# Six of eight layer norms turned by VectorE blocks and copies between partition quarters

## The chip, the cores and the metric

The kernel runs on one core of one Trainium2 chip. Its metric is the device time of one execution in microseconds (us). The core has TensorE (PE, matrix products; its weight loads are shown as PEld), VectorE (DVE), ScalarE (ACT), GpSimd (POOL) and SyncE (SP), whose queue issues nearly all transfers (DMA). Each engine works through its own instructions in the order in which the program gives them, and an instruction that waits holds up those behind it on the same engine. This holds for SP too: a transfer that waits for its data or for its buffer holds up the transfers behind it.

## The reference: what is computed

A cross-attention block with an MLP, for four batches `b`, with L = 512 rows, D = 512 features, 16 heads of 32 and an inner width of 2048, all in float32:

```
xn  = layer_norm(x) * ln1_w + ln1_b                      # LN1
q   = xn @ q_w + q_b ;  k = ctx @ k_w + k_b ;  v = ctx @ v_w + v_b
out = softmax(q k^T / sqrt(32)) v                        # per head
h   = out @ cproj_w + cproj_b + x
y   = layer_norm(h) * ln2_w + ln2_b                      # LN2
out = h + gelu(y @ fc_w + fc_b) @ proj_w + proj_b
```

There are eight layer norms, LN1(b) and LN2(b) for the four batches. Each norm has its rows (positions) on the partitions, four tiles of 128 rows by 512 features, and the products that follow want features on the partitions. So each normed batch, 512 x 512, is turned (transposed), and the norm's weight and bias are applied on the turned side, where they are one scalar per partition.

## The kernel before, in words

**Attention units.** Heads are taken in groups of four: 4 batches x 4 groups give 16 windows `w`, and each window has 4 blocks of 128 query rows, so there are 64 units `u = 4 w + qt`. A unit, in the program's order: perhaps `attend` of an earlier pair, then `scores(w, qt)` (PE into `sc`; VectorE adds the mask and takes the minimum, L284; ScalarE takes exponentials, L288), then `turn(w, qt)` (VectorE transposes the 32 x 32 blocks of the probabilities into `tb`, L302 and L310), then a list of other work that fills PE.

**Pairs and their copies.** A block transpose on VectorE turns only inside blocks of 32 x 32, that is inside a quarter of the partitions. Two units make a pair (pair `2 w + half`), and sixteen SP transfers (`copies`, L345) move its blocks between the four partition quarters from `tb` into `pT`. Then `attend` (L362, `av`) multiplies with `v`, and VectorE scales the result into `oT` (L367). Most pairs, 8 to 24 among them, share one `pT` buffer: their copies are put into SP's order by `exchange`, called in `attend` of the pair before. In the units told of here, an even unit attends pair (u - 4) / 2: unit 20 pair 8, unit 22 pair 9, unit 24 pair 10, and so on to unit 50 and pair 23.

**Filling work.** Preparations `k`, `q`, `v` of window `w` (`prep_k`, `prep_q`, `prep_v`; k9 is that of window 9), output projections `c` (`cproj`, four per batch), and the MLP of batch 0 and half of batch 1 (`fc`, `proj`). Each is one "chain" of PE. Their weights come over SP: `load_w` for `k`, `q`, `v`, two windows ahead, and `load_mlp`, eight tiles ahead. `load_x`, `load_enc` and `load_h` (L194, L189, L391) load a batch's input, context and residual. What fills which unit stands in `first[w]` and `later[w]`. A tuple gives one list for each of the window's four units. Otherwise `run` takes from one list by due times: each chain has a price (CHAIN 3.4, a group of turns TURN 0.5, other steps 0), the sum over the window is divided over its units, and a step is taken while the price spent plus half of its own is within what is due.

**Norms and turns.** `ln_stat` takes mean and variance (VectorE), `ln_rs` the inverse deviation (GpSimd), `ln_norm` the normed rows in place or into a tile of the pool `tiles` (tag `xn`, four buffers), on VectorE or, for LN1(1) and LN1(2), on ScalarE (L163). `ln_turn` then makes a quarter of the turn: four PE transposes of 128 x 128 into PSUM (L176, tile `tp`), and one pass over them with weight and bias, on ScalarE (L181) or VectorE (L179). Four of these make a norm. LN1's turned result is `xT` (a half of the tile `xe`), read by `prep_q`. LN2's is `yT`, one buffer, read by `fc` and in the last phase.

**Last phase.** After the units, `last_mlps` does the second half of batch 1's MLP and those of batches 2 and 3, with fewer products by sums of blocks (L573 and L613). LN2(2) and LN2(3) are turned there, in `project`, after its second product (`turns()`). `y_sums` and the next batch's first products read the result.

Of the kernel before, what the change touches and what calls it, by code (L numbers as in the profile page):

```python
# [1 line left out]

# [9 lines left out]
F32 = mybir.dt.float32  # L38
U8 = mybir.dt.uint8
AF = mybir.ActivationFunctionType  # L40
# [5 lines left out]
P = 128  # L46
B, L, D, H = 4, 512, 512, 16
HD = D // H
INNER = 4 * D
NT = L // P  # L50
ND = D // P
# [5 lines left out]
NI = P // HD  # L57
# [15 lines left out]
LN1W, LN1B, QB, KB, LN2W, LN2B, FCB = 0, 4, 8, 12, 16, 20, 24  # L73
# [4 lines left out]
def xattn_block(ctx: ExitStack, tc: tile.TileContext, x, encT, mask, q_w, k_w, v_w, c_w, fc_w, p_w, vecs, rows, out):  # L78
    nc = tc.nc
    scale = float(np.float32(1.0) / np.sqrt(HD).astype(np.float32))  # L80

    def pools(stack, **bufs):
        return [stack.enter_context(tc.tile_pool(name=n, bufs=k)) for n, k in bufs.items()]

    const, keep, hids, tiles, small = pools(ctx, const=1, keep=1, hids=6, tiles=4, small=4)
    dram = ctx.enter_context(tc.tile_pool(name="dram", bufs=1, space=bass.MemoryType.DRAM))
    ps_acc = ctx.enter_context(tc.tile_pool(name="ps_acc", bufs=4, space=PSUM))

# [6 lines left out]
    vec = const.tile([P, NVEC], F32, tag="vec", name="vec")  # L95
# [9 lines left out]
    eT, xT = (xe[:, i * ND * L : (i + 1) * ND * L].rearrange("p (d l) -> p d l", d=ND) for i in range(2))  # L105
# [9 lines left out]
    def k_q(w, i):  # L115
        n = w % 4 * 2 + i
        return pbt[:, n * D : (n + 1) * D]
# [11 lines left out]
    def kqv_w(w, i):  # L129
        n = 4 * i + 2 + w % 2  # L130
        return ptt[:, n * D : (n + 1) * D].rearrange("p (d f) -> p d f", d=ND)

    S = {}
    count = [0, 0, 0]
    Q = [nc.sync]

    def acc_tile(name):
        return ps_acc.tile([P, D], F32, tag="acc", name=name)


    def ln_stat(key, t, src):
        if t == 0:
            S["mv", key] = small.tile([P, NT, 2], F32, tag="mv", name=f"mv{key[0]}_{key[1]}")
        st = small.tile([P, 6], F32, tag="st", name=f"st{key[0]}_{key[1]}_{t}")
        nc.vector.bn_stats(st, src)
        nc.vector.bn_aggr(S["mv", key][:, t, :], st)

    def ln_rs(key):

        ve = small.tile([P, NT], F32, tag="ve", name=f"ve{key[0]}_{key[1]}")  # L150
        nc.gpsimd.tensor_scalar(ve, S["mv", key][:, :, 1], EPS, 1.0, ALU.add, ALU.mult)
        rs = small.tile([P, NT], F32, tag="rs", name=f"rs{key[0]}_{key[1]}")
        nc.gpsimd.tensor_tensor(rs, ve, nhalf, ALU.pow)
        S["rs", key] = rs
        if key in BY_ACT:
            nm = small.tile([P, NT], F32, tag="nm", name=f"nm{key[0]}_{key[1]}")
            nc.gpsimd.tensor_tensor(nm, S["mv", key][:, :, 0], rs, ALU.mult)
            nc.gpsimd.tensor_scalar(nm, nm, -1.0, 0.0, ALU.mult, ALU.add)
            S["nm", key] = nm

    def ln_norm(key, t, dst, src):
        if key in BY_ACT:
            nc.scalar.activation(  # L163
                dst, src, AF.Identity, bias=S["nm", key][:, t : t + 1], scale=S["rs", key][:, t : t + 1]
            )
            return
        nc.vector.tensor_scalar(
            dst, src, S["mv", key][:, t, 0:1], S["rs", key][:, t : t + 1], ALU.subtract, ALU.mult
        )

    def ln_turn(key, d, xn, dst):

        w, bi = (LN1W, LN1B) if key[0] == 1 else (LN2W, LN2B)
        tp = acc_tile(f"tp{key[0]}_{key[1]}_{d}")
        for t in range(NT):
            nc.tensor.transpose(tp[:, ts(t, P)], xn[t][:, ts(d, P)], ident)  # L176
        wd, bd = vec[:, w + d : w + d + 1], vec[:, bi + d : bi + d + 1]
        if d in (1, 2) and key not in BY_ACT:
            nc.vector.tensor_scalar(dst[:, d, :], tp, wd, bd, ALU.mult, ALU.add)  # L179
        else:  # L180
            nc.scalar.activation(dst[:, d, :], tp, AF.Identity, bias=bd, scale=wd)  # L181


    def queue(b):
        return Q[0] if b else nc.sync

    def load_enc(b):
        for d in range(ND):
            queue(b).dma_start(out=eT[:, d, :], in_=encT[b, ts(d, P), :])  # L189

    def load_x(b):
        S["xn", b] = [tiles.tile([P, D], F32, tag="xn", name=f"xn1_{b}_{t}") for t in range(NT)]
        for t in range(NT):
            queue(b).dma_start(out=S["xn", b][t], in_=x[b, ts(t, P), :])  # L194

# [11 lines left out]
    def ln1_turn(b, d):  # L207
        ln_turn((1, b), d, S["xn", b], xT)
# [167 lines left out]
    def stays(b, t):  # L376

        return b == 0 or b == SPLIT and t < 2

    def load_h(b, *ts_):  # L380

        if ("xa", b) not in S:
            S["xa", b] = dram.tile([L, D], F32, tag=f"xa{b}", name=f"xa{b}")
        for t in ts_:
            if b == B - 1:

                S["h", b, t] = k_q(t // 2, t % 2)
            else:
                pool, tag = (hids, "hid") if stays(b, t) else (tiles, "xn")
                S["h", b, t] = pool.tile([P, D], F32, tag=tag, name=f"h_{b}_{t}")  # L390
            Q[0].dma_start(out=S["h", b, t], in_=x[b, ts(t, P), :])  # L391
            if stays(b, t):
                S["hid", b, t] = S["h", b, t]
# [14 lines left out]
    def load_xn(b):  # L408

        for t in range(NT):  # L410
            S["h", b, t] = tiles.tile([P, D], F32, tag="xn", name=f"hn_{b}_{t}")
            Q[0].dma_start(out=S["h", b, t], in_=S["xa", b][ts(t, P), :])

    def load_hid(b, ts_):
# [8 lines left out]
    def stat2(b, t):  # L423
        ln_stat((2, b), t, S["h", b, t])

    def norm2(b, t):
        h = S["h", b, t]
        y = tiles.tile([P, D], F32, tag="xn", name=f"xn2_{b}_{t}") if stays(b, t) else h
        S.setdefault(("yn", b), {})[t] = y
        ln_norm((2, b), t, y, h)  # L430

    def proj_bias(b):
        for t in range(NT):
            if stays(b, t):
                add_row(S["hid", b, t], 1)

    def ln2_turn(b, d):
        if d == 0:
            S["yT", b] = keep.tile([P, ND, L], F32, tag="yT", name=f"yT_{b}")
        ln_turn((2, b), d, S["yn", b], S["yT", b])  # L440


    weights, products = [], []
# [268 lines left out]
    CHAIN, TURN = 3.4, 0.5  # L712

    def do(fn):
        return [(0.0, fn)]

    def A(w):
        if w >= NW:
            return []
        return [  # L720
            (CHAIN, lambda: prep_k(w)),
            (CHAIN, lambda: prep_q(w)),
            (CHAIN, lambda: prep_v(w)),
        ]

    def C(b):
        return [(CHAIN, lambda t=t: cproj(b, t)) for t in range(NT)]

    def turns1(b):
        return [(TURN, lambda d=d: ln1_turn(b, d)) for d in range(ND)]  # L730

    def turns2(b):
        return [(TURN, lambda d=d: ln2_turn(b, d)) for d in range(ND)]

    def FC(b, q):
        return [(CHAIN, lambda f=f: fc(b, f)) for f in range(q * FQ, (q + 1) * FQ)]
# [3 lines left out]

    def inputs(b):
        ln = [(0.0, lambda part=part: ln1(b, part)) for part in range(3)]
        return do(lambda: load_x(b)), ln, turns1(b), do(lambda: load_enc(b))

    def run(work, budget=None):

# [33 lines left out]
    x1, x2, x3, x4 = inputs(1)  # L780
# [9 lines left out]
    first = [[] for _ in range(NW)]  # L790
    later = [[] for _ in range(NW)]
# [17 lines left out]
    def some(n):  # L809
        taken, mlp[:n] = mlp[:n], []  # L810
        return taken
# [4 lines left out]
    def h_(b, *ts_):  # L816
        return do(lambda: load_h(b, *ts_))
# [4 lines left out]
    def pb_(b):  # L822
        return do(lambda: proj_bias(b))

    def rs(b):
        return do(lambda: ln_rs((2, b)))

    def stat(b, *ts_):
        return do(lambda: [stat2(b, t) for t in ts_])

    def norm(b, *ts_):
        return do(lambda: [norm2(b, t) for t in ts_])


    x1, x2, x3, x4 = inputs(2)
    k, q, v = A(7)
    c, t2 = C(0), turns2(0)
    first[4] = x1 + [k, q, v] + x4
    later[4] = c[:1] + x2[:1] + c[1:2] + x2[1:2] + c[2:3] + x2[2:] + c[3:]
    k, q, v = A(8)  # L840
    first[5] = (
        [k] + stat(0, 0, 1, 2, 3) + rs(0) + x3 + norm(0, 0, 1, 2, 3) + [v], [q] + t2, some(2) + pb_(0), some(2)
    )
    k, q, v = A(9)
    x1, x2, x3, x4 = inputs(3)
    first[6] = [k, q] + some(4) + [v] + x1
    k, q, v = A(10)
    first[7] = [k, q] + x2[:1] + some(2) + x2[1:2] + some(3) + [v]

    k, q, v = A(11)  # L850
    first[8] = h_(1, 0, 1) + x2[2:] + [k, q] + x3[:2] + some(1) + x3[2:3] + [v] + x3[3:] + h_(1, 2, 3) + x4
    later[8] = cb(1) + C(1)
    k, q, v = A(12)
    first[9] = [q] + some(2) + [k] + some(2) + [v]
    k, q, v = A(13)
    first[10] = [k, q] + some(4) + [v]
    k, q, v = A(14)
    t2 = turns2(1)
    first[11] = (
        [k, q] + stat(1, 0, 1, 2, 3) + rs(1), some(2) + norm(1, 0, 1, 2, 3), some(1) + t2[:2] + [v],  # L860
        t2[2:] + pb_(1) + some(1) + h_(2, 2, 3, 0, 1)
    )

    k, q, v = A(15)
    c = C(2)
# [49 lines left out]
    c = C(B - 1)  # L915
# [49 lines left out]
```

## Time and profile before

| | |
|---|---|
| median of 3 runs | 810.5 us (809.81 to 810.87) |
| span of the profiled execution | 810.8 us |
| PE busy | 794.0 us (98%) |
| VectorE, ScalarE, GpSimd busy | 556.1, 359.8, 98.5 us |
| PE transposes of the norms (L176) | 128 instructions, 16 a norm |
| copies of pairs on SP into `pT` (L345) | 384 transfers of 136 KB, 2.4 us from issue to landing |

Times inside the execution are microseconds from the start of the span. A line of the profile names an engine, the source line (L176), the operation and the tiles as out<-in; `[4.15 <-ACT pbt L248]` says that the engine had been idle for 4.15 us and that the operation named ended this. PEclk is TensorE's granted clock, in tenths of full speed. SPq is SP's queue of transfers. The units told of below start, by their `av`, at 153.17 us (unit 20), 196.94 (unit 24), 266.32 (unit 32), 304.38 (unit 36), 389.69 (unit 46) and 421.47 (unit 50).

### The profile page before, as it was taken

What the parts mean: (1) busy time and instruction counts of PE and PEld (TensorE: products, weight loads), DVE (VectorE), ACT (ScalarE), POOL (GpSimd) and SP (SyncE); (2) the same over time, 40 slices, a digit from 0 to 9 for tenths busy, and PEclk for the clock granted to TensorE, in tenths of its full rate; (3) what the DMA queues carried; (4) which work ended last, traced back from release to release, by engine and by line L of the source; (5) the groups of instructions that cost most, each with busy time, mean ns of one, the idle gap of its engine ahead of it and who ended that gap; (6) DMA issues with size and microseconds to landing.
All of it is one profiled execution on the core that took longest, in us unless ns stands there. A gap on an engine that the chain in (4) does not pass through costs nothing.

```text
span 810.8 us, 11918 instructions
## 1 busy us (share of the span) xinstructions
PE 794.0 (98%) x4082; PEld 482.1 (59%) x4082; DVE 556.1 (69%) x1273; ACT 359.8 (44%) x785; POOL 98.5 (12%) x112
## 2 busy tenths in 40 slices
PE   9999999979999999999999999999999999999998
PEld 6545445444354544535554333445888888888887
DVE  3779998876678765867778998636738993358511
ACT  2557765537673646546644469700312330023200
POOL 1110030030000030001131000120050021200011
PEclk9999999989999999999999999999999999999999
DMA  9899999937797877778668798883335330023001
GB/s 332 277 236 221 236 223 243 243 92 186 186 240 173 229 202 201 168 196 210 165 144 219 192 266 222 214 247 127 97 111 175 111 116 14 27 79 91 1 14 39
DMA packets 60956, 137.14 MB, mean 169 GB/s; under 512 B 12464, under 2 KB 15664, under 8 KB 60768
## 3 DMA queue, kind: packets, MB, share of 16 engines
q1 hardware_dynamic: 59472, 132.43, 61.3%
q0 software_dynamic: 896, 2.82, 1.0%
q10 hardware_dynamic: 528, 1.14, 0.6%
q8 instruction: 32, 0.52, 0.3%
q14 instruction: 28, 0.23, 0.1%
HBM read 58.22 MB, written 6.82 MB: 80 GB/s over the span
## 4 chain that ended last, share of the span: by engine, by line
PE 82%; DVE 7%; SPq 4%; ACT 3%; DMA 3%; issue 1%; POOL 0%; DVEq 0%; POOLq 0%; ACTq 0%
PE q L573 15%; PE accf L469 7%; PE accc L403 7%; PE sc L279 7%; PE acck L235 6%; PE av L362 6%; PE accp L479 6%; PE accv L257 6%; PE accq L245 6%; SPq L345 4%; DVE ptt L284 2%; PE q5p L613 2%; PE q3p L613 2%; PE q7p L613 2%; PE q2p L613 2%; PE q6p L613 2%
## 5 line engine op out<-in xcount | busy, mean ns | idle before, releaser
L288 ACT ACTIVATE ptt<-ptt,mn 128x512 f32<-128x512 f32 x256 | 181.6, 711 | 134.2 <-DVE mn L284 134.1
L284 DVE CUSTOM_DVE_ANT_0 ptt<-sc,mb 128x512 f32<-128x512 f32 x256 | 161.1, 685 | 47.5 <-PE sc L279 47.4
L302 DVE STREAM_TRANSPOSE tb<-ptt 128x512 f32<-128x512 f32 x224 | 142.0, 683 | 5.5 <-ACT ptt L288 5.1
L469 PE MATMUL accf<-yT,pbt 128*128 128x512 f32 x192 | 87.3, 602 | 0.0
L479 PE MATMUL accp<-pbt,gt 128*128 128x512 f32 x192 | 86.7, 600 | 0.3 <-DMA pbt<-p_w_dram 0.3
L279 PE MATMUL sc<-pbt 32*128 32x512 f32 x512 | 73.7, 645 | 5.2 <-ACT pbt L248 2.7
L573 PE MATMUL q<-ys,gt 128*128 128x256 f32 x320 | 75.1, 379 | 0.0
L573 PEld LDWEIGHTS q<-ys,gt 128*128 128x128 f32 x320 | 60.9, 190 | 8.2
L469 PEld LDWEIGHTS accf<-yT,pbt 128*128 128x128 f32 x192 | 35.0, 190 | 50.2 <-issue 45.4
L479 PEld LDWEIGHTS accp<-pbt,gt 128*128 128x128 f32 x192 | 35.2, 190 | 49.3 <-issue 45.6
L257 PEld LDWEIGHTS accv<-ptt,xe 128*128 128x128 f32 x512 | 58.9, 192 | 8.2 <-issue 6.9
L257 PE MATMUL accv<-ptt,xe 128*128 128x128 f32 x512 | 60.5, 277 | 0.0
L245 PE MATMUL accq<-xe,ptt 128*128 128x512 f32 x128 | 59.3, 607 | 0.0
L235 PE MATMUL acck<-xe,ptt 128*128 128x512 f32 x128 | 59.3, 606 | 0.0
L573 PE MATMUL q<-yT,gt 128*128 128x256 f32 x240 | 58.1, 380 | 0.5 <-DVE gt L501 0.5
L403 PE MATMUL accc<-wc,oT 128*128 128x512 f32 x128 | 56.6, 596 | 0.0
L269 POOL TENSOR_TENSOR v<-v,row 128x512 f32<-128x512 f32 x16 | 20.4, 1272 | 281.4 <-ACT v L262 281.3
L577 ACT ACTIVATE ga<-uc,vec 128x256 f32<-128x256 f32 x40 | 20.3, 508 | 75.5 <-DVE uc L551 75.5
L573 PEld LDWEIGHTS q<-yT,gt 128*128 128x128 f32 x240 | 45.6, 190 | 7.4 <-DVE gt L501 0.9
L362 PE MATMUL av<-pT,v 128*32 128x256 f32 x768 | 48.1, 393 | 1.5 <-DMA pT<-tb 1.5
L584 ACT COPY p<-q 128x256 f32<-128x256 f32 x20 | 7.1, 353 | 92.0 <-PE q L573 92.0
L288 ACT ACTIVATION_READ_ACCUMULATOR ptt<-ptt,mn 128x1 f32 x256 | 47.8, 187 | 0.0
(121 smaller groups left out, 940.4 us busy)
## 6 DMA issues: line engine op xcount, KB each, us to landing
pT<-tb SPq DMA_DIRECT2D x384, 136.0 KB, 2.4
pbt<-p_w_dram SPq DMA_DIRECT2D x40, 256.0 KB, 3.2
gt<-fc_w_dram SPq DMA_DIRECT2D x40, 256.0 KB, 2.7
gt<-tb SPq DMA_DIRECT2D x64, 136.0 KB, 2.8
xe<-tb SPq DMA_DIRECT2D x56, 136.0 KB, 3.1
pbt<-fc_w_dram SPq DMA_DIRECT2D x24, 256.0 KB, 4.7
ptt<-k_w_dram SPq DMA_DIRECT2D x16, 256.0 KB, 3.8
xe<-encT_dram SPq DMA_DIRECT2D x16, 256.0 KB, 4.3
```

The costliest lines, as they stand in the source:

```text
L235: nc.tensor.matmul(acc, S["wk", w][:, d, :], eT[:, d, :], start=(d == 0), stop=(d == ND - 1))
L245: nc.tensor.matmul(acc, S["wq", w][:, d, :], xT[:, d, :], start=(d == 0), stop=(d == ND - 1))
L257: nc.tensor.matmul(acc[:, ts(t, P)], eT[:, d, ts(t, P)], S["wv", w][:, d, :], start=(d == 0), stop=(d == ND - 1),)
L279: nc.tensor.matmul(sc[:, h, :], qT[r, ts(qt, P)], kT[r, :], start=True, stop=True)
L284: nc.vector.tensor_tensor_reduce(out=s, in0=sc[:, h, :], in1=S["mb", w // NG], scale=1.0, scalar=FMAX, op0=ALU.add, op1=ALU.min, accum_out=mn,
L288: nc.scalar.activation(s, s, AF.Exp, bias=mn, scale=-1.0, accum_out=sums[:, qt, h : h + 1])
L302: nc.vector.transpose(tv[:, q, h], S["ps", w, qt][h])
L362: nc.tensor.matmul(av[ts(h, HD), : 2 * P].rearrange(shape, **kw), v[:, t, ts(h, HD)], p[t][h], start=(t == 0), stop=(t == NT - 1),)
L403: nc.tensor.matmul(acc, S["oT", b][:, g, ts(t, P)], wc[:, g, :], start=(g == 0), stop=(g == NG - 1))
L469: nc.tensor.matmul(acc, S["fcw", b, f][:, d, :], S["yT", b][:, d, :], start=(d == 0), stop=(d == ND - 1))
L479: nc.tensor.matmul(acc, gT[q % 2][:, k, ts(t, P)], S["pw", b, q * FQ + k], start=(k == 0), stop=(k == FQ - 1))
L573: nc.tensor.matmul(o, a[:, k], y[:, k], start=(k == 0), stop=(k == 1))
```

## The change

LN1(0) and LN1(1) stay as they are. For LN1(2), LN1(3) and all four LN2, the turn is made in three steps:

- `ln_flip`: four VectorE transposes (128 x 512 each) turn the 32 x 32 blocks of the normed rows into the destination (`xT` or `yT`).
- `ln_swap`: sixteen SP transfers, each of 32 partitions by 2 KB, move these blocks between the partition quarters, from the destination back into the ring of normed rows. That ring is now one fixed tile `xnt` of four slots instead of a pool.
- `ln_affine`: four ScalarE passes (128 x 512) apply weight and bias, from `xnt` into the destination.

So a norm's ring is in use until its last ScalarE pass; before, it was free after PE's transposes. The steps' prices in the due times are 0, where four groups of turns had 0.5 each.

The order of units 16 to 47 changes with this. Worked out by the due times, the filling work is:

| unit | before | after |
|---|---|---|
| 16, 17 | k7 q7; v7 | k7; q7 v7 |
| 18, 19 | c0 c1; c2 c3 | c0; c1 c2 |
| 20 | k8, statistics of LN2(0), turns of LN1(2), norm of LN2(0), v8 | flip LN1(2), c3, statistics, k8, swap LN1(2) |
| 21 | q8, turns of LN2(0) | a statistic, affine LN1(2), v8 |
| 22 | fc0 fc1 | norm and flip LN2(0), q8, v9, swap LN2(0) |
| 23 | fc2 fc3 | affine LN2(0), k9, q9 |
| 24 to 27 | k9 q9; fc4 fc5; fc6; fc7 v9 | fc0 fc1; fc2 fc3; fc4; fc5 fc6 |
| 28 to 31 | k10 q10; proj0 proj1; proj2 proj3; fc8 v10 | k10 q10; fc7 proj0; proj1 proj2; proj3 v10 |
| 32 | `load_h` (2), norm LN1(3), k11, q11, a turn | the same, flip LN1(3) in place of the turn |
| 33 | turn, fc9, turn, v11 | fc8, swap LN1(3), v11, affine LN1(3), `load_h` (2), `load_enc` |
| 34 | turn, `load_h` (2), `load_enc`, c0, c1 | c0, c1 |
| 36 to 38 | q12 fc10; fc11 k12; proj4 | q12 fc9; fc10 fc11; k12 proj4 |
| 46 | proj8, two turns of LN2(1), v14 | flip LN2(1), proj8, v14, swap LN2(1) |
| 47 | two turns, proj9, `load_h` (4) | affine LN2(1), proj9, `load_h` (4) |

In the last phase, flip, swap and affine of LN2(2) and LN2(3) stand at the place of the turns. The core of the diff:

```diff
-    const, keep, hids, tiles, small = pools(ctx, const=1, keep=1, hids=6, tiles=4, small=4)
+    const, keep, hids, small = pools(ctx, const=1, keep=1, hids=6, small=4)
...
+    xnt = const.tile([P, NT * D], F32, tag="xnt", name="xnt")
+
+    def xn_tile():
+        n = count[3] % NT
+        count[3] += 1
+        return xnt[:, n * D : (n + 1) * D]
...
+    def ln_flip(key, xn, dst):
+
+        tmp = dst.rearrange("p d l -> p (d l)").rearrange("p (j c t q) -> p t c j q", j=NI, c=ND, t=NT)
+        for t in range(NT):
+            nc.vector.transpose(tmp[:, t], xn[t])
+
+    def ln_swap(dst):
+
+        tmp = dst.rearrange("p d l -> p (d l)").rearrange("p (j n) -> p j n", j=NI)
+        for d in range(NI):
+            for i in (0, 2, 1, 3):
+                j = (i + d) % NI
+                nc.sync.dma_start(out=xnt[ts(j, HD), ts(i, D)], in_=tmp[ts(i, HD), j])
+
+    def ln_affine(key, dst):
+
+        w, bi = (LN1W, LN1B) if key[0] == 1 else (LN2W, LN2B)
+        raw = xnt.rearrange("p (i c t q) -> p c t i q", i=NI, c=ND, t=NT)
+        for d in range(ND):
+            nc.scalar.activation(
+                dst[:, d, :].rearrange("p (t i q) -> p t i q", t=NT, i=NI), raw[:, d], AF.Identity,
+                bias=vec[:, bi + d : bi + d + 1], scale=vec[:, w + d : w + d + 1],
+            )
...
-    def ln2_turn(b, d):
-        if d == 0:
+    def ln2_turn(b, step):
+        if step == 0:
             S["yT", b] = keep.tile([P, ND, L], F32, tag="yT", name=f"yT_{b}")
-        ln_turn((2, b), d, S["yn", b], S["yT", b])
+            ln_flip((2, b), S["yn", b], S["yT", b])
+        elif step == 1:
+            ln_swap(S["yT", b])
+        else:
+            ln_affine((2, b), S["yT", b])
...
     k, q, v = A(7)
+    k8, q8, v8 = A(8)
+    k9, q9, v9 = A(9)
     c, t2 = C(0), turns2(0)
     first[4] = x1 + [k, q, v] + x4
-    later[4] = c[:1] + x2[:1] + c[1:2] + x2[1:2] + c[2:3] + x2[2:] + c[3:]
-    k, q, v = A(8)
+    later[4] = c[:1] + x2[:1] + c[1:2] + x2[1:2] + c[2:3] + x2[2:]
     first[5] = (
-        [k] + stat(0, 0, 1, 2, 3) + rs(0) + x3 + norm(0, 0, 1, 2, 3) + [v], [q] + t2, some(2) + pb_(0), some(2)
+        x3[:1] + c[3:] + stat(0, 0, 1, 2) + [k8] + x3[1:2], stat(0, 3) + rs(0) + x3[2:] + [v8],
+        norm(0, 0, 1, 2, 3) + t2[:1] + [q8, v9] + t2[1:2], t2[2:] + pb_(0) + [k9, q9]
     )
-    k, q, v = A(9)
     x1, x2, x3, x4 = inputs(3)
-    first[6] = [k, q] + some(4) + [v] + x1
+    first[6] = some(7) + x1
...
-    first[8] = h_(1, 0, 1) + x2[2:] + [k, q] + x3[:2] + some(1) + x3[2:3] + [v] + x3[3:] + h_(1, 2, 3) + x4
+    first[8] = h_(1, 0, 1) + x2[2:] + [k, q] + x3[:1] + some(1) + x3[1:2] + [v] + x3[2:] + h_(1, 2, 3) + x4
...
-        [k, q] + stat(1, 0, 1, 2, 3) + rs(1), some(2) + norm(1, 0, 1, 2, 3), some(1) + t2[:2] + [v],
+        [k, q] + stat(1, 0, 1, 2, 3) + rs(1), some(2) + norm(1, 0, 1, 2, 3), t2[:1] + some(1) + [v] + t2[1:2],
         t2[2:] + pb_(1) + some(1) + h_(2, 2, 3, 0, 1)
     )
```

In units 20 to 22, `x3` is the list flip, swap, affine of LN1(2), `t2` that of LN2(0), and `some(n)` takes the next n steps of the MLP.

More of the change, by code (lines that the diff above doesn't have):

```diff
@@ L131, in kqv_w @@
         return ptt[:, n * D : (n + 1) * D].rearrange("p (d f) -> p d f", d=ND)
+    xnt = const.tile([P, NT * D], F32, tag="xnt", name="xnt")
[3 more added lines that the diff above has]
+        return xnt[:, n * D : (n + 1) * D]
     S = {}
-    count = [0, 0, 0]
+    count = [0, 0, 0, 0]
     Q = [nc.sync]
@@ L191, in load_x @@
     def load_x(b):
-        S["xn", b] = [tiles.tile([P, D], F32, tag="xn", name=f"xn1_{b}_{t}") for t in range(NT)]
+        S["xn", b] = [xn_tile() for t in range(NT)]
         for t in range(NT):
@@ L388, in load_h @@
             else:
-                pool, tag = (hids, "hid") if stays(b, t) else (tiles, "xn")
-                S["h", b, t] = pool.tile([P, D], F32, tag=tag, name=f"h_{b}_{t}")
+                S["h", b, t] = hids.tile([P, D], F32, tag="hid", name=f"h_{b}_{t}") if stays(b, t) else xn_tile()
             Q[0].dma_start(out=S["h", b, t], in_=x[b, ts(t, P), :])
@@ L410, in load_xn @@
         for t in range(NT):
-            S["h", b, t] = tiles.tile([P, D], F32, tag="xn", name=f"hn_{b}_{t}")
+            S["h", b, t] = xn_tile()
             Q[0].dma_start(out=S["h", b, t], in_=S["xa", b][ts(t, P), :])
@@ L427, in norm2 @@
         h = S["h", b, t]
-        y = tiles.tile([P, D], F32, tag="xn", name=f"xn2_{b}_{t}") if stays(b, t) else h
+        y = xn_tile() if stays(b, t) else h
         S.setdefault(("yn", b), {})[t] = y
@@ L730, in turns1, with flips1 @@
         return [(TURN, lambda d=d: ln1_turn(b, d)) for d in range(ND)]
+    def flips1(b):
+        return [
+            (0.0, lambda: ln_flip((1, b), S["xn", b], xT)),
+            (0.0, lambda: ln_swap(xT)),
+            (0.0, lambda: ln_affine((1, b), xT)),
+        ]
     def turns2(b):
-        return [(TURN, lambda d=d: ln2_turn(b, d)) for d in range(ND)]
+        return [(0.0, lambda n=n: ln2_turn(b, n)) for n in range(3)]
     def FC(b, q):
@@ L742, in inputs @@
         ln = [(0.0, lambda part=part: ln1(b, part)) for part in range(3)]
-        return do(lambda: load_x(b)), ln, turns1(b), do(lambda: load_enc(b))
+        return do(lambda: load_x(b)), ln, turns1(b) if b < 2 else flips1(b), do(lambda: load_enc(b))
     def run(work, budget=None):
@@ L850, in xattn_block @@
     k, q, v = A(11)
-    first[8] = h_(1, 0, 1) + x2[2:] + [k, q] + x3[:2] + some(1) + x3[2:3] + [v] + x3[3:] + h_(1, 2, 3) + x4
+    first[8] = h_(1, 0, 1) + x2[2:] + [k, q] + x3[:1] + some(1) + x3[1:2] + [v] + x3[2:] + h_(1, 2, 3) + x4
     later[8] = cb(1) + C(1)
     k, q, v = A(12)
-    first[9] = [q] + some(2) + [k] + some(2) + [v]
+    first[9] = [q] + some(3) + [k] + some(2) + [v]
     k, q, v = A(13)
```

## The prediction

> **What bounds the kernel now.** I read the page's busy shares first, then TensorE's own instructions in order of time, then the SP queue's, and last the rows of single operations.
>
> ```profile
> span 810.8 us, 11918 instructions
> PE 794.0 (98%) x4082; PEld 482.1 (59%) x4082; DVE 556.1 (69%) x1273; ACT 359.8 (44%) x785; POOL 98.5 (12%) x112
> PEclk9999999989999999999999999999999999999999
> ```
>
> TensorE (PE) is busy nearly all the time, so whatever it no longer does is a gain, unless it waits instead. Its instructions in order of time show the one long wait in the units that the change rearranges:
>
> ```profile
> 166.13 3.70 PE L245 MATMUL accq<-xe,ptt 128*128 128x512 f32 x8
> 169.67 0.49 PE L176 MATMUL tp<-ident,xn 128*128 128x128 f32 x3
> 170.70 1.20 PE L176 MATMUL tp<-ident,xn 128*128 128x128 f32 x9 [0.54 <-DVE xn L167]
> 176.05 1.11 PE L176 MATMUL tp<-ident,xn 128*128 128x128 f32 x4 [4.15 <-ACT pbt L248]
> 177.10 3.22 PE L362 MATMUL av<-pT,v 128*32 128x256 f32 x28
> ```
>
> The turns of LN2(0) wait 0.54 + 4.15 us, and the `av` behind them takes about 3.6 us instead of 1.86: the granted clock is 0.50 from 176 to 179 us. A wait of 1.94 us at 48.7 us has the same sequel (clock 0.55; `sc` 1.86 instead of 1.07, `accq` 4.6 instead of 3.5), while after 1.63 us at 84.5 the clock stays at 1.00. So a wait of about 2 us or more costs some 1.7 us on top.
>
> The SP queue in order of time (start, length, line, transfer, count):
>
> ```profile
> 135.41 1.82 SPq L194 DMA_DIRECT2D xn<-x_dram  x4
> 138.28 12.29 SPq L345 DMA_DIRECT2D pT<-tb  x16
> 151.24 1.87 SPq L189 DMA_DIRECT2D xe<-encT_dram  x4
> 155.62 10.99 SPq L345 DMA_DIRECT2D pT<-tb  x16
> ...
> 288.31 10.02 SPq L345 DMA_DIRECT2D pT<-tb  x16
> 298.43 1.26 SPq L391 DMA_DIRECT2D h<-x_dram  x2
> 299.75 1.85 SPq L189 DMA_DIRECT2D xe<-encT_dram  x4
> ...
> 392.15 10.06 SPq L345 DMA_DIRECT2D pT<-tb  x16
> 402.57 1.78 SPq L391 DMA_DIRECT2D h<-x_dram  x4
> 409.54 25.09 SPq L345 DMA_DIRECT2D pT<-tb  x32
> ```
>
> A pair's sixteen copies hold this queue for 10.0 to 12.3 us, land 1.8 us after the last issue (2.4 us from issue to landing, of which 0.6 is the issue), and start 2.45 us after the previous `av` (153.17 to 155.62), because there is one `pT`. From one `av` to the next that makes 2.45 + 10 + 1.8 = 14.3 us; PE brings 14.6 to 18.1 us of work for it. Nothing of 7 us fits between two pairs' copies without PE waiting at `av`. That is what I build on.
>
> **PE's own saving.** One norm's sixteen turns take 1.96 us (592.13 to 594.09, by PE's rows). Six norms: about 11.6 us. If the wait at 170 us goes too, that is 0.54 + 4.15 + 1.7 = 6.4 us more.
>
> **The new work, each norm.** Four VectorE transposes (0.62 us apart, as at L302) are 2.5 us, in place of two evacuations of 0.80 (none in LN1(2)). Four ScalarE passes 0.73 apart (L163's, 128x512 from SBUF) are 2.9 us, in place of two or four of 0.77. Both engines have the room (69% and 44% busy): I cost them at nothing except where they stand in the chain below. In the two norms of the last phase everything is hidden: turned around 592, data 7.4 + 1.8 + 2.9 us later is there by 605, and first read by PE near 609. If that cover failed, each would cost its excess.
>
> **The swap.** Sixteen transfers of 32 rows of 2 KB have no row. Shortest issue on SP: 0.33 us, so 16 x 0.33 = 5.3 us; same shape but 4.25 KB rows (the copies): 10.0 us. I take 2 KB rows as the nearer, the x loads' 1.82 / 4 = 0.46 us, so S = 7.4 us, and keep both ends. After the last issue 1.8 us to land.
>
> [...]
>
> **Units 16 to 24** (times as in the profile). The fourth output projection (c3, 3.53 us) moves behind `av` of pair 8, and PE arrives there at 153.17 - 3.53 = 149.6. But that `av` needs copies that end on SP at 150.57; moving one weight load behind them gains 0.5, so they land at 150.1 + 1.8 = 151.9: PE waits 2.3 us, and 1.7 for the clock. Then unit 20 (`av`, `sc`, two chains: 10.0), unit 21 (4.6): `av` of pair 9 at 168.2, q8 due at 171.1. Meanwhile SP: copies 9 from 151.9 + 2.45 = 154.3, 11.0 us beside the encoder loads, to 165.3; a weight load to 165.9; the swap of LN1(2) to 173.3, landed 175.1; first ScalarE pass 0.8 later. q8 starts at 175.9: a wait of 4.8, and 1.7 for the clock. ScalarE stands in that wait too, in order: behind the four passes (178.0) come v8's evacuation (178.6) and the exponentials of unit 22 (181.4), then on VectorE the last transpose (182.0), the norm of LN2(0) (4 x 0.54, 184.1), its flip (186.6); then SP swaps to 194.0 (copies 10 are through at 183.7), landed 195.8, first pass 196.6. PE: q8, v9, unit 23 (8.1), `av`, `sc`: ready for fc0 at 195.7, so fc0 starts at 196.6. Before, PE starts k9 at 199.87 with one chain (3.53) more behind it, which units 36 to 39 catch up. Net +0.3: the waits eat the whole gain of two norms and of the old wait. With S = 5.3 it is -1.8, with 10.0 it is +7.2. The three preparations k9, q9, v9 that move earlier bring weight loads of 0.4 to 0.6 us each, in the gap after copies 10; the MLP's products from fc0 on, and their weight loads, come one chain later until unit 39, past no copies that wait for them.
>
> **Units 32 to 36.** In the order written by the due times, the swap of LN1(3), and also `load_h` (2 loads) and the encoder load (4), now stand in unit 33, ahead of pair 16's copies (before, behind them: 288.31, then 298.43). The loads overwrite the ring that the ScalarE passes read, so SP stands until those are done. From `av` of pair 14: fc8 ends at 14.6 and its weight load at 15.0; swap to 22.4; landed 24.2; passes to 27.1; two loads 28.0; four 29.9; copies 11.0 (beside loads) 40.9; landed 42.7. PE's work to that `av`: 10.0 + 8.1 + 10.0 + 8.1 = 36.3. Wait 6.4, clock 1.7, less the turns' 1.9: +6.2.
>
> **Units 46 to 50.** From `av` of pair 21: copies 22 from 2.5 to 12.5; the swap of LN2(1) to 19.9; landed 21.7; passes to 24.6; four `h` loads, which wait for the passes, 26.4; copies 23 (10.5) 36.9; landed 38.7. PE gets to that `av` after 10.0 + 4.6 + 10.0 + 4.6 = 29.2. Wait 9.5, clock 1.7, less turns 1.8 and the old wait there 0.3: +9.1.
>
> **Sum**: +0.3 + 6.2 + 9.1 - 3.9 (two last norms) = +11.7, on 810.5: 822. The profiled span of 810.8 lies 0.3 above the median.
>
> [...]
>
> **Bounds of this case.** S = 5.3: -1.8 + 4.1 + 7.0 - 3.9 = +5.4; without the clock's price twice (3.4) and with copies of 10.0 us (1.5), +0.5: 811. S = 10: +7.2 + 8.8 + 11.7 - 3.9 = +23.8: 834.
>
> **Rivals.**
> 1. *The swap is cheap on SP* (the other side). The last pair's sixteen copies, eight on SP and eight on ScalarE's queue, take 7.17 us; at that rate 2 KB rows take 7.17 x 2 / 4.25 = 3.4. With S = 3.4 q8 waits 0.8 us and fc0 starts at 190.0: -6.3; units 32 to 36 +2.2 (a wait of 2.4), units 46 to 50 +5.1, the end -3.9: -2.9, 808. It decides below S = 4.1, the zero between -2.9 and +5.4. Against it: no SP issue is under 0.33 us, so one queue needs 5.3.
> 2. *The queue is no obstacle*: PE's saving counts in full, 810.5 - 11.6 - 6.4 = 792.5. For it: the PE share of 98%. Against it: `av` waits for `pT` at 370 (1.17) and 421 (0.33) even now, with less on the queue.
> 3. *The swaps cost what the copies do*: 834. For it: same shape and direction. Against it: half the bytes.
>
> **How the numbers follow.** The likeliest (SP delays `av`, 811 to 830) gets 0.67, rival 3 0.14, rival 1 0.13, rival 2 0.05, and 0.01 is left. Within 0.2% (1.6 us, about what a measurement can tell from no change) fall only the low end of the likeliest and a part of rival 1: 0.04. Faster 0.15, slower 0.81. The range runs from 808 to 834.
>
> **What would show it.** In the profile after: no turns on PE for six norms; sixteen swap transfers of 5 to 10 us on SP, each behind a pair's copies; waits of PE before q8 (3 to 7 us, released by ScalarE) and at `av` in units 36 and 50 (4 to 9 and 8 to 12 us, released by the DMA into `pT`); SP waiting for ScalarE before the `h` loads of units 33 and 47; the granted clock near 0.5 after each wait; the turns gone at 592 and 674 without a wait. The prediction is wrong if issues are much shorter than 0.33 us each, or if the copies of pairs 16 and 23 start right after `av` of pairs 15 and 22 as now.

## The result

The changed kernel takes **845.88 us** (median of four runs, 841.59 to 846.09), and the kernel before, measured beside it, 810.68 us (809.81 to 813.12): a ratio of 1.0419, with a 95% interval from 1.0399 to 1.0439. The forecast was 822.0, with a range of 808 to 834. Its direction held, its size did not.

The page of the changed kernel, the lines that answer to those shown of before:

```profile
span 844.3 us, 11860 instructions
PE 789.4 (93%) x3986; PEld 474.1 (56%) x3986; DVE 562.3 (67%) x1287; ACT 364.9 (43%) x793; POOL 97.7 (12%) x112
PEclk9999999969999997999996999999999999999999
PE 72%; SPq 12%; DMA 6%; DVE 6%; issue 1%; ACT 1%; ACTq 0%; DVEq 0%
```

PE issues 96 matmuls fewer, six norms of sixteen. Its busy time falls by 4.6 us only, since matmuls after a wait ran at a lower granted clock (6, 7 and 6 in PEclk; its mean over the span is 0.972, before 0.994). Its time not busy grows from 16.8 (810.8 less 794.0) to 54.9 us. The last line is the chain that ended last: SP's queue holds 12% of it, 4% before.

TensorE's rows in order of time, the waits over 2 us that the kernel before does not have (start, length, then in brackets how long PE waited and for what):

```profile
172.20 3.51 PE L368 MATMUL av<-pT,v 128*32 128x256 f32 x32 [5.67 <-DMA pT<-tb]
183.27 6.58 PE L251 MATMUL accq<-xe,ptt 128*128 128x512 f32 x8 [6.49 <-ACT xe L185]
206.89 7.13 PE L478 MATMUL accf<-yT,pbt 128*128 128x512 f32 x16 [2.39 <-ACT yT L185]
324.76 3.64 PE L368 MATMUL av<-pT,v 128*32 128x256 f32 x32 [14.46 <-DMA pT<-tb]
457.38 3.64 PE L368 MATMUL av<-pT,v 128*32 128x256 f32 x32 [12.68 <-DMA pT<-tb]
```

These are `av` of pair 9, q8, fc0, and `av` of pairs 16 and 23. Three of them wait for copies on SP, two for the ScalarE passes that end a norm's turn. And SP's queue:

```profile
158.75 11.30 SPq L351 DMA_DIRECT2D pT<-tb  x16
170.78 10.02 SPq L178 DMA_DIRECT2D xnt<-xe  x16
181.53 10.03 SPq L351 DMA_DIRECT2D pT<-tb  x16
193.89 10.66 SPq L178 DMA_DIRECT2D xnt<-yT  x16
...
289.14 13.17 SPq L178 DMA_DIRECT2D xnt<-xe  x16
306.91 0.81 SPq L396 DMA_DIRECT2D xnt<-x_dram  x2
307.77 1.85 SPq L195 DMA_DIRECT2D xe<-encT_dram  x4
309.72 29.21 SPq L351 DMA_DIRECT2D pT<-tb  x32
...
427.55 10.04 SPq L178 DMA_DIRECT2D xnt<-yT  x16
442.16 1.76 SPq L396 DMA_DIRECT2D xnt<-x_dram  x4
...
629.67 10.01 SPq L178 DMA_DIRECT2D xnt<-yT  x16
```

L178 is the swap. It takes 10.0 us where nothing disturbs it, as long as the copies (L351), which move 2.1 times the bytes (136 KB a transfer for 64). The forecast had 7.4.

Where the time went can be read by laying the two traces side by side at places with the same work behind them: `sc` of unit 15 (120.20 before, 121.18 after), `av` of pair 14 (266.32, 273.82; after has one chain of 3.53 us still to do there), of pair 18 (337.35, 363.20), of pair 24 (444.31, 482.50), and the last product's start (800.54, 834.01).

| stretch | forecast, us | measured, us |
|---|---|---|
| up to unit 15, not touched | 0 | +1.0 |
| units 16 to 31 | +0.3 | +10.0 |
| units 32 to 39 | +6.2 | +14.8 |
| units 40 to 51 | +9.1 | +12.3 |
| the rest, with the two last norms | -3.9 | -4.7 |
| sum | +11.7 | +33.5 |

### The profile page after: what moved, and what is told of

Same layout as the page of the kernel before. It is cut to its first block, busy times and chain, and to the rows that moved or that the text cites. A ratio compares the mean times of both kernels' runs of the same rounds, so it can differ in the third digit from the quotient of the medians.

```text
span 844.3 us, 11860 instructions
## 1 busy us (share of the span) xinstructions
PE 789.4 (93%) x3986; PEld 474.1 (56%) x3986; DVE 562.3 (67%) x1287; ACT 364.9 (43%) x793; POOL 97.7 (12%) x112
## 3 DMA queue, kind: packets, MB, share of 16 engines
q10 hardware_dynamic: 528, 1.14, 0.6%
## 4 chain that ended last, share of the span: by engine, by line
PE 72%; SPq 12%; DMA 6%; DVE 6%; issue 1%; ACT 1%; ACTq 0%; DVEq 0%
PE q L582 14%; PE accf L478 8%; SPq L351 8%; PE accp L488 8%; PE av L368 6%; PE sc L285 5%; PE accv L263 5%; PE accq L251 5%; PE acck L241 4%; PE accc L408 4%; SPq L178 4%; DVE ptt L290 3%; PE q5p L622 2%; PE q7p L622 2%; PE q6p L622 2%; PE q2p L622 2%
## 5 line engine op out<-in xcount | busy, mean ns | idle before, releaser
L308 DVE STREAM_TRANSPOSE tb<-ptt 128x512 f32<-128x512 f32 x224 | 143.7, 686 | 35.9 <-ACT ptt L294 35.5
L368 PE MATMUL av<-pT,v 128*32 128x256 f32 x768 | 51.4, 413 | 34.8 <-DMA pT<-tb 34.2
L251 PE MATMUL accq<-xe,ptt 128*128 128x512 f32 x128 | 63.1, 638 | 6.5 <-ACT xe L185 6.5
L368 PEld LDWEIGHTS av<-pT,v 128*32 128x32 f32 x768 | 25.2, 117 | 63.3 <-issue 49.0
L251 PEld LDWEIGHTS accq<-xe,ptt 128*128 128x128 f32 x128 | 25.2, 203 | 42.1 <-issue 31.3
L373 DVE TENSOR_TENSOR oT<-av,pT 128x256 f32<-128x256 f32 x24 | 10.1, 420 | 57.7 <-PE av L368 48.5
```

What stands on the lines that cost most here:

```text
L251: nc.tensor.matmul(acc, S["wq", w][:, d, :], xT[:, d, :], start=(d == 0), stop=(d == ND - 1))
L308: nc.vector.transpose(tv[:, q, h], S["ps", w, qt][h])
L368: nc.tensor.matmul(av[ts(h, HD), : 2 * P].rearrange(shape, **kw), v[:, t, ts(h, HD)], p[t][h], start=(t == 0), stop=(t == NT - 1),)
```

## The experiments

The theory (A): SP's time for the swaps, and what stands behind them on SP, makes the waits, and without it the saved turns are a gain. The rivals (B and others, as each text has them): the order of the work, the one tile `oT`, or the new chain itself (flip, swap, passes) costs the time. All ratios are to the kernel before, measured beside each.

**1. The tile `oT` fixed.** The rows that raised it, of the changed kernel, in order of time on PE and then VectorE:

```profile
151.62 1.93 PE L368 MATMUL av<-pT,v 128*32 128x256 f32 x32 [0.83 <-DMA pT<-tb]
153.49 1.14 PE L285 MATMUL sc<-pbt 32*128 32x512 f32 x8
154.56 3.70 PE L408 MATMUL accc<-wc,oT 128*128 128x512 f32 x8
```
```profile
158.29 0.42 DVE L373 TENSOR_TENSOR oT<-av,pT 128x256 f32<-128x256 f32 x1 [5.62 <-PE accc L408]
```

`oT` has one buffer. The chain c3, moved behind `av` of pair 8, still reads batch 0's, so the scaling of pair 8 into the next batch's `oT` waits for c3 to end; it reads `pT` too, so copies 9 start at 158.75 and not near 154. The experiment drops the new tile for each batch:

```diff
-            S["oT", b] = one.tile([P, NG, L], F32, tag="oT", name=f"oT_{b}")
+            S["oT", b] = S["oT", 0] if b else one.tile([P, NG, L], F32, tag="oT", name="oT")
```

> The changed kernel, with the scaled attention output oT of all batches kept in one fixed tile, so that pair 8's scaling waits only for the columns that it writes and not for all readers of batch 0's output. Theory A (the output projection c3, moved behind av of pair 8, still reads the only oT buffer when pair 8's result is to be written; so pT comes free and pair 9's copies start about 4 us late): the scaling of pair 8 follows its av by about 2.4 us, pair 9's copies start near 154 us instead of 158.75, PE's wait at av of pair 9 falls from 5.7 us to under 1.5, all that follows comes some 4.5 us earlier, 840 to 842 us. Rival (pair 9's copies are late because VectorE is busy with statistics in front of the scaling, or because of SP): no change, 846 us.

Measured: 842.69 us, 1.039 [1.0358, 1.0422]. Two rows of it:

```profile
153.84 10.04 SPq L351 DMA_DIRECT2D pT<-tb  x16
...
166.11 10.01 SPq L178 DMA_DIRECT2D xnt<-xe  x16
```
```profile
178.59 6.76 PE L251 MATMUL accq<-xe,ptt 128*128 128x512 f32 x8 [8.05 <-ACT xe L185]
```

Copies 9 start 4.9 us earlier, and the wait at `av` of pair 9 falls from 5.67 to 1.24. But q8 now waits 8.05 instead of 6.49: PE comes to it earlier than the swap gains. The mechanism is shown (VectorE's statistics, the rival, held nothing up once the tile was fixed); its worth in time (3 us, with intervals that overlap) is not larger than what a comparison can tell.

**2. Loads behind the copies.** In units 33 and 47 the loads into the ring and of the context stood ahead of a pair's copies and waited for the ScalarE passes.

```diff
-    first[8] = h_(1, 0, 1) + x2[2:] + [k, q] + x3[:1] + some(1) + x3[1:2] + [v] + x3[2:] + h_(1, 2, 3) + x4
-    later[8] = cb(1) + C(1)
+    first[8] = h_(1, 0, 1) + x2[2:] + [k, q] + x3[:1] + some(1) + x3[1:2] + [v] + x3[2:]
+    later[8] = h_(1, 2, 3) + x4 + cb(1) + C(1)
...
-        t2[2:] + pb_(1) + some(1) + h_(2, 2, 3, 0, 1)
+        t2[2:] + pb_(1) + some(1)
...
-    first[12] = [k, q], cb(2) + [v], c[:2], c[2:]
+    first[12] = h_(2, 2, 3, 0, 1) + [k, q], cb(2) + [v], c[:2], c[2:]
```

> The changed kernel, with the loads that wait for the ScalarE passes put behind the next pair's copies: load_h (2) and load_enc of unit 33 to the head of unit 34's list, load_h (4) of unit 47 to the head of unit 48's. The swaps stay where they are. Theory A (SP stands at these loads until the passes are done, and the copies of pairs 16 and 23 stand behind them): copies 16 start right after the swap, near 303 instead of 309.7 us, and copies 23 near 438 instead of 444; PE's waits at those av fall from 14.5 and 12.7 us to 4 to 7 each, 828 to 836 us. Rival (the swap's own hold of SP makes these waits alone): each wait falls by 2 us at most, 842 us or more.

Measured: 827.82 us, 1.0215 [1.0183, 1.0247]. SP's queue and PE's two waits:

```profile
287.08 12.94 SPq L178 DMA_DIRECT2D xnt<-xe  x16
300.75 10.03 SPq L351 DMA_DIRECT2D pT<-tb  x16
310.87 1.01 SPq L396 DMA_DIRECT2D xnt<-x_dram  x2
```
```profile
313.08 3.53 PE L368 MATMUL av<-pT,v 128*32 128x256 f32 x32 [4.95 <-DMA pT<-tb]
438.90 3.64 PE L368 MATMUL av<-pT,v 128*32 128x256 f32 x32 [6.00 <-DMA pT<-tb]
```

Six and four loads, 2.7 and 1.8 us of issue, had cost about half of the loss (1.0419 to 1.0215), because SP stood at them for ScalarE's passes (302.94 to 306.91 in the changed kernel's unit 33, 437.59 to 442.16 in unit 47) while the copies waited behind. What is left at these two places is put down to the swap itself; the second run of experiment 4 tests this.

**3. The swap in four wide transfers.** The same bytes in 4 transfers of 128 partitions by 2 KB. They do not exchange the quarters, so this step of the computation is left out.

```diff
-        for d in range(NI):
-            for i in (0, 2, 1, 3):
-                j = (i + d) % NI
-                nc.sync.dma_start(out=xnt[ts(j, HD), ts(i, D)], in_=tmp[ts(i, HD), j])
+        for i in range(NI):
+            nc.sync.dma_start(out=xnt[:, ts(i, D)], in_=tmp[:, i])
```

> The changed kernel, with each swap made of four transfers of 128 partitions by 2 KB instead of sixteen of 32 partitions by 2 KB: the same bytes, but the quarters are not exchanged, so six of the eight norms' results are not the reference's. Theory A (SP pays per transfer, about 0.6 us each, whatever its bytes; this is what was mis-sized): a swap holds SP for 2 to 2.5 us instead of 10, the waits before q8 and fc0 are gone, those at av of pairs 16 and 23 fall to 2 to 5 us, the one at av of pair 9 (5.7 us) stays, 808 to 816 us. Rival (the swap is bound by the bytes that it moves between partitions): it holds SP or lands as late as before, 840 us or more.

Measured: 822.27 us, 1.0146 [1.0109, 1.0183].

```profile
168.25 2.46 SPq L176 DMA_DIRECT2D xnt<-xe  x4
173.79 10.07 SPq L349 DMA_DIRECT2D pT<-tb  x16
185.09 2.62 SPq L176 DMA_DIRECT2D xnt<-yT  x4
```
```profile
169.67 3.60 PE L366 MATMUL av<-pT,v 128*32 128x256 f32 x32 [5.61 <-DMA pT<-tb]
304.01 3.64 PE L366 MATMUL av<-pT,v 128*32 128x256 f32 x32 [7.42 <-DMA pT<-tb]
431.44 3.64 PE L366 MATMUL av<-pT,v 128*32 128x256 f32 x32 [6.65 <-DMA pT<-tb]
```

A transfer of 256 KB holds SP for 0.6 us (2.46 / 4), as one of 64 KB (10.02 / 16) and one of 136 KB (10.03 / 16) do. So the swap cost SP here by the number of transfers, not by bytes (10.0 us in sixteen, 2.46 in four), and the waits at q8 and fc0 are gone or under 0.6. The wait at pair 9 stays, as the `oT` reading wants. Those at 16 and 23 halve only, since the loads still stand ahead of the copies: they start at 286.56 and 415.53, after ScalarE's passes, the copies at 290.32 and 417.34. Theory A had not counted this, and the experiment came out slower than it said.

**4. Both repairs, and then the swaps off SP.** First the edits of 1 and 2 together:

> The changed kernel with both edits: oT in one fixed tile, and the loads that wait for the ScalarE passes behind the next pair's copies. Theory A (the two waits are separate; what is left is the swaps' own 10 us on SP): the gains add, 3 and 18 us, 823 to 826 us; left are PE's waits before q8 (about 8 us), fc0 (2 to 3) and at av of pairs 16 and 23 (5 to 6 each). Rival (the waits stand in for each other, a removed one comes back at the next): 828 us or more.

Measured: 826.51 us, 1.0198 [1.0171, 1.0225], with 7.80 us of waiting at q8, 4.19 at pair 16 and 6.16 at pair 23. Beside experiment 2 (1.0215), the gain of the `oT` edit again can't be told from none. Then the same with the swap's transfers issued by GpSimd:

```diff
-                nc.sync.dma_start(out=xnt[ts(j, HD), ts(i, D)], in_=tmp[ts(i, HD), j])
+                nc.gpsimd.dma_start(out=xnt[ts(j, HD), ts(i, D)], in_=tmp[ts(i, HD), j])
```

> The changed kernel with oT in one tile and the loads behind the copies, and with the swaps' transfers issued by GpSimd instead of SP. Theory A (the loss left is SP's time of 0.63 us per transfer, in which the pairs' copies stand): copies 16 and 23 start right after av of the pair before, PE's waits there go to under 2 us each, and the swap of LN1(2) need not wait for copies 9; if GpSimd's issues take about 0.55 us each as its stores do, 806 to 814 us. Rival (the copies' and the swaps' data hinder each other, or GpSimd issues far slower than SP): waits before q8 and fc0 as long as now or longer, 822 us or more.

Measured: 809.85 us, 0.9983 [0.996, 1.0007]: the whole loss is gone, 1.0198 to 0.9983 of it by the queue alone. GpSimd's rows, and PE's three largest waits behind unit 16 (the profiled execution took 814.45 us, the longest of ten):

```profile
190.43 4.96 POOL L178 DMA_DIRECT2D xnt<-yT  x10
...
406.98 7.96 POOL L178 DMA_DIRECT2D xnt<-yT  x16
```
```profile
154.69 3.64 PE L368 MATMUL av<-pT,v 128*32 128x256 f32 x32 [4.60 <-DMA pT<-tb]
179.54 5.40 PE L251 MATMUL accq<-xe,ptt 128*128 128x512 f32 x8 [3.41 <-ACT xe L185]
201.36 7.13 PE L478 MATMUL accf<-yT,pbt 128*128 128x512 f32 x16 [1.78 <-ACT yT L185]
```

GpSimd issued a transfer in 0.50 us (4.96 / 10, 7.96 / 16), so even here a swap lasts 8 us, but no copy waits behind it. The first of the three waits is not the swaps': in this execution copies 8 hold SP from 140.49 for 12.27 us, to 152.76 (to 147.11 in the run before), ahead of any swap. The other two are, and with the clock lost at q8 (5.40 for 3.70) they cost 6.9 us. Waits of 0.5 to 1.3 us stand at six other places. Together they take a good part of what six norms (11.6) and the old wait (6.4) would give back; a full account of the rest stays open.

**5. The order without the swaps.** The changed order with the four norms of the attention units turned on PE, all sixteen transposes at the place of the ScalarE passes (shown for LN1; `ln2_turn` does the same for batches 0 and 1):

```diff
-            (0.0, lambda: ln_flip((1, b), S["xn", b], xT)),
-            (0.0, lambda: ln_swap(xT)),
-            (0.0, lambda: ln_affine((1, b), xT)),
+            (0.0, lambda: None),
+            (0.0, lambda: None),
+            (0.0, lambda: [ln1_turn(b, d) for d in range(ND)]),
```

> The changed kernel's order of the units, but the four norms of the attention phase turned on TensorE at the place of the ScalarE passes; only LN2(2) and LN2(3) by flip and swap. Theory A (the loss is the swaps on SP, not the order): the long waits before q8, fc0 and at av of pairs 16 and 23 are gone; left are the old wait's removal (-6.4), the saved turns of the last phase (-3.9), and the wait at av of pair 9 that c3 makes (+4 to +7 with the clock), 805 to 812 us. Rival (the order itself brings the loss, by c3 and by the loads ahead of copies 16): 820 us or more.

Measured: 826.57 us, 1.0192 [1.0163, 1.0221], which is not what theory A expected. The waits at q8, fc0 and at pairs 16 and 23 are gone, as it says, but there are three others:

```profile
172.29 6.38 PE L263 MATMUL accv<-ptt,xe 128*128 128x128 f32 x32 [7.17 <-ACT xe L163]
195.54 6.67 PE L241 MATMUL acck<-xe,ptt 128*128 128x512 f32 x8 [3.77 <-ACT yT L163]
418.46 3.70 PE L493 MATMUL accp<-pbt,gt 128*128 128x512 f32 x8 [3.77 <-ACT yT L163]
```

L163 is the pass that empties PE's transposes. Sixteen turns in a row take all four PSUM buffers that the chains use too, and the next chain waits until ScalarE has emptied one. ScalarE has the exponentials of the next unit ahead of these passes, and before the first wait's end it stands idle for 4.29 us in front of them, until VectorE is ready. The kernel before spreads the turns over a window. So the test put in a cost of its own, and **what the order alone is worth in the changed kernel stays open**. The last kernel of experiment 4 has the same order but for ten loads, and is level with the kernel before: the order doesn't have to bring the loss. This run says in passing that the old way of turning has a price too once it isn't spread.

**6. Only the last phase** (b1 in the texts below). The kernel before, with only LN2(2) and LN2(3) turned in the new way:

```diff
-        ln_turn((2, b), d, S["yn", b], S["yT", b])
+        if b < 2:
+            ln_turn((2, b), d, S["yn", b], S["yT", b])
+        elif d == 0:
+            ln_flip((2, b), S["yn", b], S["yT", b])
+        elif d == 1:
+            ln_swap(S["yT", b])
+        elif d == 2:
+            ln_affine((2, b), S["yT", b])
```

> The kernel before, with only LN2(2) and LN2(3), the two of the last phase, turned by flip, swap and affine; order of the units as before. Theory A (there the swap's 10 us lie beside PE's products and no copies stand behind it): the turns' 1.96 us are saved twice, 806.5 to 807.5 us. Rival (the longer way of the data makes y_sums or the next products wait): 810 us or more.

Measured: 808.0 us, 0.9956 [0.9939, 0.9973], by the ratio 3.6 us of gain for two norms of 1.96. No copies stand behind these swaps, and their 10.0 us on SP each (590.01 to 600.03, 671.43 to 681.44) did not show in the time.

**7. The old wait at 170 us.** Experiment 6, with k9, q9 and v9 made some units earlier to fill that wait. In the first form, k9 and q9 go into a buffer that units 22 and 23 still read, so the values that those two units work on are changed; the work is the same.

> The kernel before, with LN2(2) and LN2(3) by flip, swap and affine, and with another order in units 20 to 27: k9, q9 and v9 come earlier (units 21 and 22), LN2(0) is normed in unit 21 and turned on TensorE in unit 22, the MLP begins in unit 23. Theory A (the wait of 4.7 us and its clock price of 1.7 at 170 us came from the norm standing too near its turns): that wait is gone and no other takes its place, 6 us under the variant with the last phase alone, 801 to 803 us. Rival (the wait moves to the new place of the turns or to av of pair 9): 806 us or more.

Measured: 798.66 us, 0.9852 [0.9826, 0.9878]. The second form (b4 in the text of experiment 8) puts them behind those units:

```diff
-        [k] + stat(0, 0, 1, 2, 3) + rs(0) + x3 + norm(0, 0, 1, 2, 3) + [v], [q] + t2, some(2) + pb_(0), some(2)
+        [k] + stat(0, 0, 1, 2, 3) + rs(0) + x3 + [v], [q] + norm(0, 0, 1, 2, 3), [v9] + t2 + pb_(0), [k9, q9]
...
-    first[6] = [k, q] + some(4) + [v] + x1
+    first[6] = some(7) + x1
```

> The kernel before with the two layer norms of the last phase turned without TensorE (as in b1) and with the tiles k, q and v of window 9 made earlier, but none ahead of the last reader of the buffer it overwrites; no other norm is changed. Theory A (the swaps of the last phase are hidden and worth two turns on TensorE, the order takes away the old wait at 170 us, 4.7 us in the profile of before with 1.7 of lost clock): b1's 808.0 less 5 to 7, 801 to 803 us, and no gap over 2 us on TensorE between 160 and 180 us. Theory B (the order only moves the wait to another unit): 806 to 809 us, with a new gap of 3 us or more before 240 us.

Measured: **799.87 us, 0.9854 [0.9829, 0.9879]**, faster than both kernels. The page, and PE's rows at the place of the old wait of 0.54 + 4.15 us:

```profile
span 796.6 us, 11897 instructions
PE 785.1 (99%) x4050; PEld 477.1 (60%) x4050; DVE 555.4 (70%) x1277; ACT 360.4 (45%) x787; POOL 97.8 (12%) x112
```
```profile
167.91 1.93 PE L393 MATMUL av<-pT,v 128*32 128x256 f32 x32
169.77 1.14 PE L310 MATMUL sc<-pbt 32*128 32x512 f32 x8
170.84 3.84 PE L288 MATMUL accv<-ptt,xe 128*128 128x128 f32 x32
174.52 2.12 PE L183 MATMUL tp<-ident,xnt 128*128 128x128 f32 x16
```

v9 (L288) now stands where PE waited, and LN2(0)'s turns find their rows ready. No wait over 1 us has come in its place in the attention units. The gain over experiment 6 (0.9956 to 0.9854, 8 us) is some 2 us more than the 6.4 of the old wait and its clock. Where the rest comes from stays open; the clock may have a part in it, since the wait of 1.94 us near 48 us has a lower clock behind it in the profile of before (`sc` 1.86 us) and not in this one (1.14).

**8. Two more norms, on GpSimd.** The last kernel, with LN1(3) and LN2(1) turned in the new way as well, their swaps on GpSimd and the loads behind the copies:

> b4, with two more layer norms (LN1(3) and LN2(1)) turned without TensorE, their swaps issued by GpSimd and the loads of the units around them put behind the copies. Theory A (what made the changed kernel slow is SP's time for the swaps and what it delays, so a swap on GpSimd leaves the saved turns as a gain): b4 less 1 to 4 us, 797 to 801 us. Theory B (a norm turned by VectorE and a swap comes too late for its reader whichever queue issues it): b4 plus 2 to 10 us, with gaps of 3 us or more at the attention products of pairs 16 or 23.

Measured: 801.09 us, 0.9865 [0.9843, 0.9888], between what the two theories expected and not to be told from the kernel without them. PE saves 32 transposes, 3.9 us, and has these waits in exchange:

```profile
152.77 1.93 PE L393 MATMUL av<-pT,v 128*32 128x256 f32 x32 [1.02 <-DMA pT<-tb]
293.99 2.63 PE L393 MATMUL av<-pT,v 128*32 128x256 f32 x32 [2.11 <-DVE h L434]
400.88 1.93 PE L393 MATMUL av<-pT,v 128*32 128x256 f32 x32 [1.53 <-DMA pT<-tb]
```

## Why the prediction was right and wrong

**Right: what bounds it.** That a pair's copies leave no room on SP, that PE would wait at `av` and not be freed, and the places q8, fc0, pairs 16 and 23 with their releasers, are all in the trace. SP stood at the loads of units 33 and 47 as said. Rival 1 (cheap swaps) is out by the swap's 10.0 us on SP, and rival 2 (the queue is no obstacle) by experiment 4: taking the swaps off SP, together with the repairs of experiments 1 and 2, gives back all of the loss (1.0419 to 0.9983). PE's saving (96 matmuls) and the last phase are right too: no wait there, -4.7 for -3.9 in the trace, and 3.6 us alone (experiment 6).

**Wrong: the size, +33.5 us of span for +11.7.** The step that failed first is the swap, "I take 2 KB rows as the nearer, the x loads' 1.82 / 4 = 0.46 us, so S = 7.4 us". It measured 10.0. The nearer row was the copies', from SBUF to SBUF in 32 partitions; the bytes made no difference to SP (experiment 3: 0.6 us a transfer of 256 KB as of one of 64). Rival 3 had this S, with the chance 0.14, and its sum of 834 was the range's upper end; the result is beyond it, so S isn't all. Stretch by stretch:

- *Units 16 to 31, 9.7 us over the forecast.* By the prediction's own working S = 10 makes 6.9 of it (+7.2 in place of +0.3). The rest goes with a wait it had excluded: "copies 9 from 151.9 + 2.45 = 154.3" missed that c3, moved behind `av` of pair 8, still reads the one `oT`. They started at 158.75, and PE waited 5.67 us at pair 9, with the clock lost after it (3.51 for 1.93). The wait of 2.3 us that was forecast at pair 8 came out as 0.83, without loss of clock.
- *Units 32 to 39, 8.6 over.* S = 10 makes 2.6. The swap there took 13.17, another 3.2: SP waited inside it for 2.4, and the last transfer took 1.64 instead of 0.59. The waits of SP's queue between 286 and 305 us (in total, times, longest):

```profile
SPq L178 <- DMA ptt<-k_w_dram: 1.4, 1, 1.4
SPq L178 <- DMA pbt<-fc_w_dram: 0.7, 1, 0.7
...
SPq L178 <- DMA ptt<-q_w_dram: 0.3, 1, 0.3
```

  A swap from `xe` into `xnt` has no use for a weight. In the trace SP's transfers signal eight semaphores in turn (823 of 837 share theirs with the one eight places before), and none of these 823 starts before that one has landed. Here those were weight loads from HBM, which landed 5.9, 6.2 and 7.0 us after their issue, at 293.59, 294.42 and 295.68: the swap's sixth, seventh and eighth transfers start at 293.61, 294.44 and 295.69. The copies behind, beside six loads, took 2.2 us more than the 11.0 + 1.8 forecast (309.72 to 324.76). 2.6 + 3.2 + 2.2 = 8.0: that is the wait, 14.46 for 6.4.
- *Units 40 to 51, 3.2 over.* S makes 2.6 of it, a wait of 12.68 for 9.5.
- *The clock* was forecast at 1.7 us after each long wait. It measured 1.6 to 1.7 in the three `av`, 0.3 and 0.6 more in the `sc` behind two of them, and 2.9 at q8 (6.58 for 3.70). After the shorter waits it was not regular: none at fc0 after 2.39 us, 3.0 at the same place in experiment 1 after 2.54 (10.17 for 7.13), 1.4 in experiment 8 after 2.11 (0.7 in `av`, 0.7 in `sc`). The traces of the kernel before and of the changed one show a reason: in both, each record of the granted clock starts a whole number of 3.41 us after the first (at 6.52 and 4.78 us after the start of the span). Of these steps of 3.41 us inside the span, seven at full clock had PE idle, by its rows, for 1.94 us or more (1.94 and 2.21 before; 1.94, 2.08, 2.09 and twice the whole 3.41 after), and half clock followed each; none of the others followed by full clock had more than 1.69. So it mattered there how a wait fell on these steps: the 2.39 us at fc0 fell on two (1.68 and 0.71), without loss. The prediction's bound of about 2 us fits the idle time of a step in these two traces, not the length of a wait. In experiment 5 even the 3.77 us at 418.46 cost no clock (3.70 us, as at full clock); how the waits of the experiments lie on such steps was not shown.

Two readings of the prediction were off without bearing on its sum: the shortest issue on SP in the trace of before is 0.32 us (L406, `xa<-pbt`) and not 0.33; and the first to read the turned rows in the last phase, at 609.51, is VectorE, PE following at 611.36.

So the range was too narrow because its upper end was a sum with one larger term. Two dependencies that cost little in the kernel before, one tile read by a moved step and a shared set of semaphores, stood outside it. The first can be read from the code. The second is in the trace of before too, where 727 of 741 transfers on SP share their semaphore with the one eight places ahead.

## What to carry to other kernels

A transfer inside SBUF held SP for about 0.6 us here, with 64, 136 or 256 KB alike: count the transfers, and ask what stands behind them on the same queue, before bytes or busy shares. When a step is moved, look up every tile that it still reads: with one buffer, its next writer moves too, and all that waits for that writer. Work taken off the bounding engine was a gain here where its new path had slack, in the last phase, and filling one old wait with work that was ready gave more (0.9956 to 0.9854) than the two norms turned there (1 to 0.9956).

## What the runs showed of the hardware

- A transfer from SBUF to SBUF held SP for about 0.6 us, whether it had 64 KB in 32 partitions (10.02 / 16), 136 KB in 32 (10.03 / 16), or 256 KB in 128 (2.46 / 4, experiment 3); four loads of 256 KB in a row from HBM held it for 0.46 each (1.85 / 4). GpSimd issued the 64 KB ones in 0.50 (7.96 / 16, experiment 4).
- The swap's 1 MB in 10.0 us is 105 GB/s; the same bytes in four transfers took 2.46 us of issue, 0.6 for each as before.
- In one swap of the changed kernel, transfers stood for 2.4 us (1.4 + 0.7 + 0.3) until weight loads had landed with which they share nothing but a semaphore.
- In the traces of the kernel before and of the changed one, TensorE's granted clock changed at whole steps of 3.41 us from its first record, and fell to half after each of the seven steps at full clock inside the span with 1.94 us or more of PE idle, after none with 1.69 or less.
